# A state-space mixer on one core: the product for dt and the next chunk's front work placed sooner in the order of half steps

## The chip, the cores and the metric

One core of a Trainium2 chip runs the whole kernel. The metric is the device time of one execution in microseconds. PE is the matrix engine (PEld its weight loads), DVE the vector engine, ACT the engine of activation functions, POOL the general engine, SP the engine that issues nearly all DMAs here. Each engine works through its own instructions in order and waits for the others by semaphores.

## The reference, cut to what matters

The input is 8 sequences of 512 tokens with 512 features, all float32. One decoder layer is computed: a state-space mixer, attention to a second input, and a mixture of 32 experts, with a layer norm after each. The change lies in the mixer:

```python
xz = xn @ in_proj_w;  x_main, z = split(xz)              # 1024 channels each
x_main = silu(causal_conv4(x_main))
dt, B_ssm, C_ssm = split(x_main @ x_proj_w)              # 32, 16, 16 columns
dt = softplus(dt @ dt_proj_w + dt_proj_b)                # 1024 channels
h = exp(A * dt) * h + dt * B_ssm * x_main                # step by step over the tokens, 16 states a channel
y = (sum over states of h * C_ssm + x_main * D) * silu(z)
out = y @ out_proj_w + residual
```

## The kernel before

**Chunks and half steps.** The mixer goes through 16 chunks: 8 sequences, each in two halves of 256 tokens (t=0 and t=1). In a chunk the 1024 channels are 8 tiles of 128, taken in four pairs q = 0 to 3; the 16 states are four groups g. So a chunk has 4 x 4 = 16 pair steps, each of two half steps; k = 0 to 31 counts the half steps, and pair q begins at k = 8q. A pair step multiplies dt*x by B (L453, DVE), scans (L460, DVE, one instruction over 128x2056), and in each of its half steps multiplies by C (L478, DVE) and adds up the states on PE into `py` (L482, "collect"). The decays exp(A*dt) (L436, ACT, eight a pair step) are made one pair step ahead. `h` has two buffers, so the multiplication of a pair step needs the collects of the one but last.

**What a pair needs first.** `prepare(q)` makes dt and dt*x for a pair: four matmul records for `ps_dt` (L390), softplus on ACT (L400 to L406), four DVE operations (L410 to L413), two ACT scalings of x by D (L416) and eight DMAs on SP that lay dt and dt*x out as `both` (L424). The first decays of a pair read `both` two half steps before the pair begins, the first L453 when it begins. Before the change `prepare` for the next pair stands at k = 8q + 2; at the last pair it is that of the next chunk's pair 0.

**What else runs in a chunk.** At k = 1 and 2 `back` multiplies the gated output of the chunk before by the out projection (L511), and its norm follows. At k = 3 to 6 `gate_x` projects z (L303), at k = 7 comes its silu. The next chunk's input is loaded at k = 5 and normed at k = 9; `flip_x` transposes it, `convolve` projects and convolves one channel pair (L303, ACT L323 and L329, DVE L337), silu follows, and `x_proj` makes dt, B and C (L360). Weights for `back`, `gate_x` and `convolve` come in pieces of 512 KB through two buffers `wm` (L263, SP): asking for one piece starts the load of the next. All their PSUM tiles share the two slots of tag `mm`.

**Side units.** Attention and the router of the sequence before (and keys and values of the next) are cut into small units with weights in PE microseconds. `work(k)` gives the mixer's own weight of a half step; at each half step units are taken from the list as long as their sum stays within the share of the whole. So a change of `work` also moves units. Among them: `keys` (DVE L696), `maximum` (PE L774, DVE L776), `weigh` and `gather`, `hidden`, and `pick` and `choose` for the router (L547; DVE L554 to L610 with one exponential on ACT, L557).

**Order.** A step's function issues its first engine's work and returns the rest, which is issued by the next `settle`, one step later; `dry` issues all that is left. A planner then fixes each engine's order when the program is built: it keeps to the program's order by and large, but lets work that it counts as ready pass work that it counts as waiting. `silu` is kept in the program's order, with the table loads around it.

```python
    def do(fn, *args, first=False):
        if first:
            dry()
        rest = fn(*args)
        settle()
        if rest:
            left.append(rest)
```

Of the kernel before, what the change touches and what calls it, by code (L numbers as in the profile page):

```python
# [81 lines left out]
def layers(ctx, tc, a, x1d, filld, based, xbuf):  # L82
# [111 lines left out]
    first = cp.tile([P, E], F32, name="l_first")  # L194
    nc.gpsimd.iota(first, pattern=[[CAP, E]], base=-SLOTS, channel_multiplier=0, allow_small_or_imprecise_dtypes=True)
    first = first.unsqueeze(1).to_broadcast([P, SC, E])
# [154 lines left out]
    def silu(*tiles):  # L351

        for v in tiles:
            tc.keep_in_program_order(nc.scalar.activation(v, v, AF.Silu))
        tc.keep_in_program_order(nc.scalar.preload_act_table_set(LN_EXP))
# [16 lines left out]
    def bcast(f, g):  # L372

        got = []
        for r0 in (g * NG, NST + g * NG):
            t = bcp.tile([P, NG // 2, T], F32, tag="bc", name="bc")
            for r in range(2):
                n0 = r0 + r * NG // 2
                nc.sync.dma_start(
                    t[r * HP : (r + 1) * HP], f["scr"][n0 : n0 + NG // 2, :].partition_broadcast(HP)  # L380
                )
            got.append(t.unsqueeze(1))
        return got
# [47 lines left out]
    def decays(q, g, dt, da):  # L431

        for i in range(2):
            for n in range(NG):
                j, m = n // 2, n % 2
                nc.scalar.activation(  # L436
                    da[:, i * NG + n, 1:], dt[:, i, j, :], AF.Exp, scale=aneg[:, 2 * q + i, j, g, m : m + 1]
                )

    def carry(t, q, g):  # L440

        h = p3.tile([P, 2 * NG, T + 1], F32, tag="h", name="h", bufs=2)
        nc.scalar.copy(h.rearrange("p (i n) t -> p i n t", i=2)[:, :, :, 0], last(q, g) if t else none)  # L443
        return h
# [4 lines left out]
    def scan(t, q, g, dtx, bc, da, h):  # L449

        steps = h.rearrange("p (j m) t -> p j m t", m=NG // 2)[:, :, :, 1:]
        both = [P, 4, NG // 2, T]
        nc.vector.tensor_tensor(  # L453
            steps,
            dtx.rearrange("p i j t -> p (i j) t").unsqueeze(2).to_broadcast(both),
            bc[0].to_broadcast(both),
            ALU.mult,
        )
        flat = h.rearrange("p n t -> p (n t)")
        nc.vector.tensor_tensor_scan(flat, da.rearrange("p n t -> p (n t)"), flat, 0.0, ALU.mult, ALU.add)  # L460
        if t < S // T - 1:
            nc.vector.tensor_copy(last(q, g), h.rearrange("p (i n) t -> p i n t", i=2)[:, :, :, T])  # L462
# [27 lines left out]
    def gated(q, f, py):  # L490

        f["xs"].pop(q)
        pair = f["zs"][:, 2 * q : 2 * q + 2, :]
        nc.vector.tensor_tensor(pair, pair, py, ALU.mult)
# [167 lines left out]
    def sources(b):  # L662

        st, todo = {}, []

        def begin():
            load("Wv")
            st["cT"] = cT = quad("s2", "cT")
            nc.sync.dma_start(cT, rows(a["ctx"][b]))
            st["mk"] = mk = p1.tile([P, S], U8, tag="mk", name="mk")  # L670
            nc.sync.dma_start(mk, a["mask"][b : b + 1, :].to_broadcast([P, S]))
            kept[b] = [dp.tile([S, D], F32, tag="vd", name="vd"), dp.tile([D, S], F32, tag="kd", name="kd")]

        def values(pc):
            if pc == 0:
                load("Wk")
            w, cT = loaded["Wv"], st["cT"]
            ps = dense(lambda dc: cT[:, dc, pc * P : (pc + 1) * P], lambda dc: w[:, dc, :])

            def put():  # L680
                v = p3.tile([P, D], F32, tag="row", name="v")
                nc.scalar.copy(v, ps)
                nc.sync.dma_start(kept[b][0][pc * P : (pc + 1) * P, :], v)

            return put

        def keys(oc):
            if oc == 0 and b:
                load("Wq")
            w, cT = loaded["Wk"], st["cT"]  # L690
            ps = dense(lambda dc: w[:, dc, oc * P : (oc + 1) * P], lambda dc: cT[:, dc, :])

            def put():

                k = p3.tile([P, D], F32, tag="row", name="k")
                nc.vector.scalar_tensor_tensor(k, ps, bk[:, oc : oc + 1], st["mk"], ALU.add, ALU.mult)  # L696
                nc.sync.dma_start(kept[b][1][oc * P : (oc + 1) * P, :], k)

            return put

        todo.append((0, begin, False))
        for j in range(SC):
            todo.append((3.4, lambda j=j: values(j), False))
        for j in range(DC):
            todo.append((3.4, lambda j=j: keys(j), False))
        return todo
# [284 lines left out]
    def settle():  # L991

        got = [part() for part in left]
        left[:] = [x for x in got if x]

    def dry():
        while left:
# [10 lines that stand above are left out]

    def work(k):

        front = 6.9 if k in (1, 2) else 3.4 if 3 <= k < 7 or k in (12, 15, 18, 21, 24) else 1.0 if k in (11, 26) else 0.0
        return 1.2 + front

    f = {}
# [16 lines left out]
    for i, (b, t) in enumerate(chunks):  # L1031
        nf = {}
        after = chunks[i + 1] if i + 1 < len(chunks) else None
        if t == 0:
            side, spent = units(b - 1) if b else sources(0), 0.0

            own = [work(k) for k in range(len(steps))] * 2
            whole = sum(own) + sum(x[0] for x in side)
        py = None
        for k, (q, g, ci) in enumerate(steps):  # L1040
            if ci == 0:
                if (q, g) != (CC // 2 - 1, NST // NG - 1):
                    bcn = bcast(f, (g + 1) % (NST // NG))
                else:
                    bcn = bcast(nf, 0) if after else None
            if ci == 0:
                h = carry(t, q, g)

                if k + 2 < len(steps) or after:
                    nq, ng, _ = steps[(k + 2) % len(steps)]  # L1050
                    decays(nq, ng, (f if k + 2 < len(steps) else nf)["ready", nq][0], das[(n + 1) % 2])
                scan(t, q, g, f["ready", q][1], bc, das[n % 2], h)
                n += 1
            if k % 8 == 0:
                if k:
                    gated(q - 1, f, py)
                elif old:
                    gated(CC // 2 - 1, old[2], old[3])
                py = psy.tile([P, 2, T], F32, tag="py", name="py")
            if k == 0 and old:  # L1060
                twice_x(*old[:3])
            if k in (1, 2) and old:
                do(back, k - 1, *old[:3], first=True)
            if 3 <= k < 7:
                do(gate_x, k - 3, f, first=(k == 3))
            if k == 7:
                dry()
                silu(f["zs"])
            if k % 8 == 2:
                if q + 1 < CC // 2:  # L1070
                    do(prepare, q + 1, f)
                elif after:
                    do(prepare, 0, nf)
            if after:
                if k == 5:
                    load_x(*after, nf)
                if k == 9:
                    norm_x(nf)
                if k == 11:
                    for j in range(DC // 2):  # L1080
                        do(flip_x, j, nf)
                if k in (12, 15, 18, 21):
                    do(convolve, after[1], (k - 12) // 3, nf, first=(k == 12))
                if k == 23:
                    dry()
                    silu(*nf["xs"].values())
                if k == 24:
                    do(x_proj, nf)
            if side and (k >= 3 or t and k == 0):
                at = t * len(steps) + k + 1  # L1090
                while side and spent + sum(own[:at]) <= whole * at / len(own):
                    w, fn, alone = side.pop(0)
                    spent += w
                    do(fn, first=alone)
            settle()
            collect(2 * q + ci, g, h, bc, py, f)
            if ci == 1:
                bc = bcn
            if i < 2 and k % 2:
                clear(i * E // 2 + k // 2)  # L1100
        while t and side:
            _, fn, alone = side.pop(0)
            do(fn, first=alone)
        old = (b, t, f, py)
        f = nf
# [322 lines left out]
```

## Time and profile before

| | us |
|---|---|
| median of three runs | 5627.29 (5623.35 to 5629.95) |
| profiled execution | 5630.07 |
| its span, first to last instruction | 5628.4 |
| first scan of the mixer, last scan | 83.7, 3732.1 |
| chunks with t=0, from the third sequence on (4, 6, ..., 14) | 228.7 to 236.4 each |
| chunks with t=1 (3, 5, ..., 13) | 238.5 to 243.4 each |
| one scan (L460), one multiplication by B (L453), by C (L478) | 4.44, 2.29, 1.22 |
| mean granted TensorE clock | 0.937 |

The span is that of one profiled execution; 1.7 us of that execution lie outside it. The mixer phase with attention and router beside it takes about two thirds of it, the experts the rest. Chunks are counted from 0 and begin where their first scan begins.

### The profile page before, as it was taken

The numbers are of one execution on the slowest core, as the hardware profiler recorded it, in microseconds if no ns is written. First come the engines' busy times: TensorE is split into PE (matmuls) and PEld (weight loads), VectorE is DVE, ScalarE is ACT, GpSimd is POOL, SyncE is SP. The second block draws the span as 40 slices with busy tenths as digits, with TensorE's granted clock in tenths as the row PEclk, the third lists the DMA queues.
The fourth block names the chain that finished last, engine by engine and source line by source line (L and its number), as shares of the span: only waits on it lengthen the run. The fifth ranks groups of instructions, "written<-read, shape, count | busy, mean of one in ns | idle before, by whom it ended". The sixth has DMA issues, their size and how long they took to land. (4 is left out here: it accounts for less than half of the span.)

```text
span 5628.4 us, 59369 instructions
## 1 busy us (share of the span) xinstructions
PE 4884.2 (87%) x19752; PEld 2733.3 (49%) x19752; DVE 4299.8 (76%) x5098; ACT 2494.3 (44%) x5186; POOL 546.4 (10%) x424
## 2 busy tenths in 40 slices
PE   5667889888888988888898898879899999999994
PEld 3334334434434433443443343333577777777773
DVE  5988888999889888988888988854456555555554
ACT  4454555555555555455554555523122222222223
POOL 0100002000200200200020020010111111111111
PEclk8888999999998999999999899989899999999997
DMA  6767345443634534544363454431344444444444
GB/s 203 215 209 214 96 127 180 126 119 111 207 94 120 183 110 124 161 146 112 108 215 85 130 180 117 116 115 47 135 124 125 123 119 125 125 124 125 117 119 138
DMA packets 560419, 769.78 MB, mean 137 GB/s; under 512 B 135754, under 2 KB 268394, under 8 KB 560112
## 3 DMA queue, kind: packets, MB, share of 16 engines
q1 hardware_dynamic: 522608, 680.70, 40.0%
q0 software_dynamic: 33280, 76.90, 7.0%
q10 hardware_dynamic: 4224, 8.39, 0.4%
q8 instruction: 157, 2.57, 0.2%
q14 instruction: 150, 1.23, 0.1%
HBM read 508.68 MB, written 165.05 MB: 120 GB/s over the span
## 5 line engine op out<-in xcount | busy, mean ns | idle before, releaser
L460 DVE TENSOR_TENSOR_SCAN h<-l_da,h 128x2056 f32<-128x2056 f32 x256 | 1135.8, 4437 | 14.3 <-ACT h L443 2.1
L436 ACT ACTIVATE l_da<-both,l_aneg 128x256 f32<-128x256 f32 x2048 | 867.4, 498 | 563.8 <-DVE h L460 517.2
L482 PE MATMUL py<-h,l_twice 128*64 128x256 f32 x4096 | 632.2, 413 | 132.0 <-DVE h L478 131.6
L453 DVE TENSOR_TENSOR h<-both,bc 128x2048 f32<-128x2048 f32 x256 | 584.3, 2287 | 140.0 <-PE py L482 75.9
L478 DVE TENSOR_TENSOR h<-h,bc 128x1024 f32<-128x1024 f32 x512 | 611.8, 1219 | 5.3 <-DVE l_state L462 0.6
L482 PEld LDWEIGHTS py<-h,l_twice 128*64 128x64 f32 x4096 | 305.3, 145 | 486.8 <-issue 213.2
L1208 PE MATMUL ps_h<-xT,w 128*128 128x320 f32 x1536 | 435.9, 433 | 0.0
L776 DVE TENSOR_REDUCE mx<-ps_s 128x2 f32<-128x1024 f32 x256 | 310.7, 1217 | 126.3 <-PE ps_s L774 123.8
L774 PE MATMUL ps_s<-l_ka,l_qa 64*128 64x512 f32 x1024 | 312.4, 686 | 79.1 <-DVE mx L776 67.1
L1288 POOL DMA_INDIRECT based<-y,xe x160 | 249.4, 1559 | 1317.1 <-ACT y L1311 577.6
L800 PE MATMUL ps_t<-l_qa,l_ka 64*128 64x512 f32 x1024 | 302.3, 664 | 70.2 <-ACT eT L804 35.9
L1208 PEld LDWEIGHTS ps_h<-xT,w 128*128 128x128 f32 x1536 | 292.6, 191 | 118.4 <-issue 0.8
L1229 DVE TENSOR_TENSOR hT<-ps_h,p 128x320 f32<-128x320 f32 x128 | 62.9, 491 | 374.4 <-PE ps_h L1208 374.3
L804 ACT ACTIVATE eT<-ps_t 128x1024 f32<-128x1024 f32 x256 | 259.3, 1013 | 152.9 <-PE ps_t L800 152.8
L816 PE MATMUL po<-eT,l_va 128*64 128x512 f32 x1024 | 294.1, 646 | 27.8 <-ACT eT L804 22.9
L303 PE MATMUL ps_z<-xnT,wm 128*128 128x256 f32 x1024 | 256.1, 407 | 37.8 <-DMA wm<-in_in_proj_w 36.2
L1208 PE MATMUL ps_h<-t,s 128*128 128x320 f32 x1024 | 286.1, 432 | 0.0
L511 PE MATMUL po<-wm,zs 128*128 128x512 f32 x512 | 244.5, 629 | 37.9 <-DMA wm<-in_out_proj_w 37.6
L649 POOL DMA_INDIRECT xbuf<-x2t,dest x128 | 209.7, 1638 | 672.4 <-DVE l_state L462 319.3
L711 PE MATMUL ps_p<-x2T,wa 128*128 128x512 f32 x512 | 251.8, 641 | 5.7 <-ACT x2T L878 5.4
L303 PE MATMUL ps_x<-xnT,wm 128*128 128x256 f32 x1024 | 245.4, 394 | 10.7 <-DVE xr L864 10.0
L303 PEld LDWEIGHTS ps_z<-xnT,wm 128*128 128x128 f32 x1024 | 203.1, 203 | 95.8 <-issue 53.6
(224 smaller groups left out, 7259.6 us busy)
## 6 DMA issues: line engine op xcount, KB each, us to landing
bc<-scr SPq DMA_DIRECT2D x1024, 128.0 KB
w<-in_w SPq DMA_DIRECT2D x96, 1024.0 KB
wm<-in_in_proj_w SPq DMA_DIRECT2D x128, 512.0 KB
xbuf<-zero SPq DMA_DIRECT2D x32, 1362.5 KB
xe<-xbuf SPq DMA_DIRECT2D x32, 1362.5 KB
both<-dt SPq DMA_DIRECT2D x256, 128.0 KB
both<-dtx SPq DMA_DIRECT2D x256, 128.0 KB
wm<-in_out_proj_w SPq DMA_DIRECT2D x64, 512.0 KB
```

Source lines behind the costliest of these rows:

```text
L303: nc.tensor.matmul(ps[:, i, :], w[:, dc, i * P : (i + 1) * P], f["xnT"][:, dc, :], start=(dc == 0), stop=(dc == DC - 1),)
L436: nc.scalar.activation(da[:, i * NG + n, 1:], dt[:, i, j, :], AF.Exp, scale=aneg[:, 2 * q + i, j, g, m : m + 1])
L453: nc.vector.tensor_tensor(steps, dtx.rearrange("p i j t -> p (i j) t").unsqueeze(2).to_broadcast(both), bc[0].to_broadcast(both), ALU.mult,)
L460: nc.vector.tensor_tensor_scan(flat, da.rearrange("p n t -> p (n t)"), flat, 0.0, ALU.mult, ALU.add)
L478: nc.vector.tensor_tensor(steps, steps, bc[1].to_broadcast([P, 2, NG // 2, T]), ALU.mult)
L482: nc.tensor.matmul(py[j * HP : (j + 1) * HP, c % 2, :], twice, h[:, j * 2 + m, 1:], start=False, stop=(s == (NST // NG - 1, NG // 2 - 1, 1)),)
L774: nc.tensor.matmul(ps[:, j, :], qa[r, lt * P : (lt + 1) * P], ka[r, :], start=True, stop=True)
L776: return lambda: nc.vector.tensor_reduce(mx[:, lt, :].unsqueeze(2), ps, AX.X, ALU.max) and None
L800: nc.tensor.matmul(ps[:, j, :], ka[r, kc * P : (kc + 1) * P], qa[r, :], start=True, stop=True)
L804: nc.scalar.activation(eT, ps, AF.Exp)
L816: nc.tensor.matmul(po[j * 2 * HD : (j + 1) * 2 * HD, :], va[:, kc, i, j * HD : (j + 2) * HD], eT[:, j, :], start=(kc == 0), stop=(kc == SC ...
L1208: nc.tensor.matmul(ps, w[:, n, r * P : (r + 1) * P], x[:, n, :], start=not more and n == 0, stop=n == 1, skip_group_check=more,)
```

## The change

`prepare` goes from k = 8q + 2 to k = 8q, ahead of `back` in the first pair. For the next chunk the flips go from k = 11 to 10, the four convolutions from 12, 15, 18, 21 to 11, 13, 15, 18, the silu from 23 to 20 and `x_proj` from 24 to 21; with `prepare` at k = 24 the next chunk's first dt product follows three half steps behind it instead of two. `work` is written anew to match: 1.0 for each `prepare`, which counted only at k = 26 before.

```diff
     def work(k):
 
-        front = 6.9 if k in (1, 2) else 3.4 if 3 <= k < 7 or k in (12, 15, 18, 21, 24) else 1.0 if k in (11, 26) else 0.0
+        front = 6.9 if k in (1, 2) else 3.4 if 3 <= k < 7 or k in (11, 13, 15, 18, 21) else 1.0 if k == 10 or k % 8 == 0 else 0.0
         return 1.2 + front
...
-            if k % 8 == 2:
+            if k % 8 == 0:
                 if q + 1 < CC // 2:
                     do(prepare, q + 1, f)
                 elif after:
...
-                if k == 11:
+                if k == 10:
                     for j in range(DC // 2):
                         do(flip_x, j, nf)
-                if k in (12, 15, 18, 21):
-                    do(convolve, after[1], (k - 12) // 3, nf, first=(k == 12))
-                if k == 23:
+                if k in (11, 13, 15, 18):
+                    do(convolve, after[1], (11, 13, 15, 18).index(k), nf, first=(k == 11))
+                if k == 20:
                     dry()
                     silu(*nf["xs"].values())
-                if k == 24:
+                if k == 21:
                     do(x_proj, nf)
```

## The prediction

> **What bounds the kernel now.** I began with the busy line of the page, then cut the span at the first scan of each chunk and read the windows.
>
> ```profile
> PE 4884.2 (87%) x19752; PEld 2733.3 (49%) x19752; DVE 4299.8 (76%) x5098; ACT 2494.3 (44%) x5186; POOL 546.4 (10%) x424
> ```
>
> ```profile
> 1631.50:1874.90 243.40, 212.10 (x855) 101.77 (x854) 214.25 (x232) 133.50 (x271) 2.71 (x8) 0.91 0.40 116
> 1874.90:2105.50 230.60, 202.74 (x832) 96.10 (x830) 205.03 (x189) 121.06 (x256) 36.51 (x21) 0.97 0.52 159
> ...
> sum 2834.30, PE 2473.83 PEld 1182.49 DVE 2515.44 ACT 1527.13 POOL 222.59; mean PE 206.15 PEld 98.54 DVE 209.62 ACT 127.26 POOL 18.55
> ```
>
> The columns are window, length, busy PE, PEld, DVE, ACT, POOL, then the clock and DMA. The rows are a t=1 and a t=0 chunk; the sum is over the twelve chunks 3 to 14. In them DVE works 2515.4 of 2834.3 us and PE 2473.8. So the mixer phase is DVE work with 319 us of idle DVE, 26.6 us a chunk, and PE nearly as full. The change does not alter DVE's work; it can win or lose only idle DVE time. The expert phase after 3741 us is not touched. Next, DVE's waits between 688 and 3741 us (total, times, longest):
>
> ```profile
> DVE h L453 <- PE py L482: 68.1, 58, 2.7
> DVE mx L776 <- PE ps_s L774: 50.1, 32, 3.9
> DVE h L453 <- DMA both<-dtx: 48.2, 8, 7.8
> DVE xs L337 <- ACT xs L329: 41.8, 24, 3.0
> DVE g_m L558 <- ACT g_sc L557: 36.2, 6, 9.9
> ...
> DVE dtx L410 <- ACT dtx L406: 12.6, 8, 2.0
> ```
>
> The third row is the largest single stall that hangs on `prepare`. Six of its eight are about 7 us long and sit at one place, the change from channel pair 0 to pair 1 in the t=0 chunks 4 to 14; one of 4.7 us is in the last chunk. The timelines of DVE, SP and PE around one of them:
>
> ```profile
> 1919.05 0.68 DVE L413 TENSOR_TENSOR dtx<-dt,xs 128x512 f32<-128x512 f32 x1
> 1926.91 4.50 DVE L453 TENSOR_TENSOR h<-both,bc 128x2048 f32<-128x2048 f32 x2 [7.18 <-DMA both<-dtx]
> ```
>
> ```profile
> 1917.88 1.98 SPq L424 DMA_DIRECT2D both<-dt  x3
> 1920.71 0.37 SPq L523 DMA_DIRECT2D x1d<-o  x1
> 1921.12 0.60 SPq L424 DMA_DIRECT2D both<-dt  x1
> 1921.82 2.63 SPq L424 DMA_DIRECT2D both<-dtx  x4
> 1924.55 0.55 SPq L263 DMA_DIRECT2D wm<-in_in_proj_w  x1
> ```
>
> ```profile
> 1898.59 7.13 PE L511 MATMUL po<-wm,zs 128*128 128x512 f32 x16 [1.51 <-DMA wm<-in_out_proj_w]
> 1905.65 1.12 PE L390 MATMUL ps_dt<-xd,l_w_dt 32*128 32x256 f32 x4
> ...
> 1928.43 5.38 PE L303 MATMUL ps_z<-xnT,wm 128*128 128x256 f32 x16 [3.13 <-DMA wm<-in_in_proj_w]
> ```
>
> The dt product is queued on PE behind both halves of `back` (1905.65), so dtx is ready only at 1919.7. Its eight copies leave SP until 1924.45 and land by 1926.9. DVE has nothing else. The same eight issues hold up the weight piece for the last z projection, and PE starves for 3.13 us.
>
> **The change, part by part** (gains against the profiled execution, 5630.1 us). What is moved per `prepare`: four PE matmul records (1.12 us), seven ACT operations, four DVE operations of 0.69, 0.68, 0.68, 0.68 = 2.7 us, two ACT scalings and eight SP issues of 0.61 us = 4.9 us.
>
> (a) *dt product two half steps sooner at pair 1.* It passes `back` (2 x 7.13 us of PE), so its copies can be issued at least 14 us earlier and the 48.2 us go. What is late next: in chunk 8 the collects of pair step 2 end on PE at 1918.8, when DVE arrives at 1919.7, so there is just room. Further on DVE waits at `keys` (L696 on ps_p, 1.9 to 3.1 us). DVE gets there 7.2 us earlier; PE recovers its 3.13 us gap and 1.66 us of slow matmuls behind it (5.38 against 3.72 us for the same 16 records at 1918.83), 4.8 us. So 2.4 us come back in six chunks: 48 - 14 = **34 us gained**, bounds 0 and 48.
>
> The row first: after a 3.13 us gap those 16 matmuls took 5.38 us. [...]
>
> (b) *L410 on ACT*, 12.6 us: eight short stalls behind the exponentials of pair 1. At half step 0 DVE has other work, but the ACT chain is as long. **8 us**, bounds -10 (as long again as now) and 12.6.
>
> (c) *silu and the gate's exponential.* In the t=1 chunks the silu of the next chunk's xs (k=23) meets the gate's exp (issued at k=22). ACT then changes tables back and forth while DVE waits:
>
> ```profile
> 2301.19 1.28 ACT L354 ACT_TABLE_LOAD   x1
> 2302.49 0.63 ACT L354 ACTIVATE xs<-xs 128x512 f32<-128x512 f32 x1
> 2303.14 1.28 ACT L557 ACT_TABLE_LOAD   x1
> 2304.43 0.31 ACT L557 ACTIVATE g_sc<-g_sc 128x128 f32<-128x128 f32 x1
> 2304.76 1.28 ACT L354 ACT_TABLE_LOAD   x1
> ```
>
> With the silu at k=20, and the gate's product moved by the new weights from k=22 to k=23, they lie apart. Of six waits (36.2 us, most of them 5.3) I leave 2.5 us each for the exp and its hand-over: **21 us**, bounds 0 and 31. The row: each load took 1.28 us and the next operation followed 0.02 us later. [...]
>
> (d) *Start of t=1 chunks.* DVE waits there 2.3 to 3.9 us for ps_s (seven times, 23.9 us). The four DVE operations of `prepare` (2.7 us) now fall into that hole, but its matmuls put ps_s off by 1.1 us: 1.6 x 7 = 11, of which I take **8**, bounds 0 and 19.
>
> (e) *What it costs.* The eight copies now stand on SP in front of or among the out-projection weights of `back`; SP is in order, and what waits behind them is those pieces, then bc. PE already waits for these pieces 28.3 us in 12 times, 2.4 us each. A delay of 4.9 us, passed on in full in all 15 chunks with a `back`, is 74 us; none is 0. Between them I take the row's 2.4 us: **-36**. The PSUM slot costs nothing: ps_dt holds one of two `mm` slots that `back` needs, but ACT reads it in 1.4 us while PE runs the first half of the piece (1.8 us).
>
> (f) *Flips at k=10, convolutions at 11, 13, 15, 18, product at 21, the other prepares.* Counts stay; distances between neighbours shrink from three half steps to two or three, over 14 us of DVE, longer than a convolution's chain (3.7 us PE, 0.57 and 1.1 us ACT, 2.9 us DVE). The flips now have one half step instead of two behind the norm; PE may wait there for ACT, which t=1 chunks cover (PE has waits on DVE there) and which costs up to 2 us each otherwise. Their L337 stalls (41.8 us) change places; **0**, bounds -20 and +20. The weights add 3.0 to each chunk's own sum (360.4 to 366.4 a batch), which moves side units by one half step at most places: inside these bounds.
>
> Sum: 34 + 8 + 21 + 8 - 36 = 35 us. 5630.1 - 35 = 5595; the median of the runs lies 2.8 us below the profiled execution: **5592 us**.
>
> **Rivals.** *Slower: SP blocks the weights.* If SP has the eight copies ahead of a weight piece, it first waits for DVE's dt (L424 on L412: 91.9 us in 34 times, 2.7 each), then issues for 4.9 us: PE gets 7.6 us late, 15 times, 114 us. Against 71 us of gains that is +43: 5670 us. It decides from 71 / 15 = 4.7 us a chunk. For it: just this happened to the z piece at 1924.55. Against it: two of the four pieces are asked for early, and the order on SP is planned by readiness.
>
> *No change: the stall only moves.* PE is busy 206 of 236 us, and the collects have 0.9 us of room at the stall shown. If PE hands back all of (a) as waits at L453 and L696, the other 37 us of gains face 36 of (e): about 5626 us. For it: 68 us of waits on py, the largest row. Against: PE has two starved stretches here that go.
>
> **How the numbers follow.** Forecast 0.60, slower rival 0.25, no change 0.15. A difference under 0.2% (11 us) cannot be told from none. The low end takes (e) at half and (b) to (d) at their bounds: 5549; the range reaches up past no change into the better part of the slower rival, 5645. Faster 0.60 (the forecast), within 0.2% 0.13 and slower 0.27 (the slower rival, and 0.02 of the third case).
>
> **What would show it.** Right: the 7 us waits on both<-dtx gone; L558's wait under 3 us; L410's and the ps_s wait at t=1 starts smaller; PE's wait for wm ahead of L511 grown to about 5 us. Wrong: that wait above 7 us with DVE waiting on py behind it, or L696 and py rows grown by as much as both<-dtx lost.

## The result, and the profile after

The changed kernel is slower: a median of 5800.75 us over four executions (5790.71 to 5805.19) against 5625.32 us over four of the kernel before, a ratio of 1.0309 (95% interval 1.0291 to 1.0327). The profiled execution took 5805.2 us with a span of 5803.5. The forecast was 5592, the range ended at 5645; even the slower rival (5670) fell 130 us short.

The busy line of the page after, in the same columns as before:

```profile
PE 4914.3 (85%) x19752; PEld 2736.4 (47%) x19752; DVE 4290.3 (74%) x5098; ACT 2527.8 (44%) x5204; POOL 638.3 (11%) x424
```

DVE has the same 5098 instructions and as much work (4290.3 against 4299.8 us); PE has 30 us more for the same instructions (the 512 of the out projection, L511, alone 257.5 against 244.5). ACT has 18 instructions more, all table loads. So the 175 us are waiting time of DVE. The windows cut at the first scan of each chunk show where: two single chunks (t=1, t=0), and the sum over the same twelve chunks as before.

```profile
1694.90:1945.10 250.20, 201.39 (x842) 98.02 (x841) 210.85 (x226) 135.13 (x272) 13.89 (x8) 0.91 0.40 111
1945.10:2195.20 250.10, 214.80 (x845) 99.56 (x843) 207.17 (x195) 124.97 (x258) 37.93 (x21) 0.93 0.49 148
...
sum 2983.60, PE 2496.32 PEld 1184.95 DVE 2507.31 ACT 1559.37 POOL 308.45; mean PE 312.04 PEld 148.12 DVE 313.41 ACT 194.92 POOL 38.56
```

The twelve chunks grew from 2834.3 to 2983.6 us, 149 us; DVE's idle time in them grew from 318.9 to 476.3. Of the rest, 13.7 us lie in the chunks ahead of these twelve (chunk 3 begins at 701.8 instead of 688.1) and 12 in the last chunk and what follows it. DVE's waits in the mixer phase after (total, times, longest):

```profile
DVE h L453 <- PE py L482: 186.2, 50, 12.6
DVE g_m L554 <- PE ps_l L547: 62.0, 7, 10.8
...
DVE hT L891 <- PE ps_p L711: 50.2, 21, 2.7
DVE total L847 <- ACT r L846: 26.9, 7, 5.3
...
DVE dtx L410 <- ACT dtx L406: 4.8, 6, 0.9
...
DVE g_m L558 <- ACT g_sc L557: 2.6, 7, 0.4
```

What the change aimed at is gone: no wait on both<-dtx (48.2 before), L558 down from 36.2 to 2.6, L410 from 12.6 to 4.8. In its place stand py (68.1 before), the router's logits ps_l (2.0 before) and hT (L891), the hidden values of the expert that all tokens use, which are worked out beside the router. The ps_l row has six waits of about 10 us, one in each t=1 chunk. This is DVE's timeline ahead of one of them:

```profile
2388.77 0.16 DVE L54 TENSOR_SCALAR v<-mv 128x4 f32<-128x4 f32 x1
2388.84 2.28 DVE L453 TENSOR_TENSOR h<-both,bc 128x2048 f32<-128x2048 f32 x1
...
2391.12 2.28 DVE L453 TENSOR_TENSOR h<-both,bc 128x2048 f32<-128x2048 f32 x1
...
2393.39 4.43 DVE L460 TENSOR_TENSOR_SCAN h<-l_da,h 128x2056 f32<-128x2056 f32 x1
...
2397.79 4.43 DVE L460 TENSOR_TENSOR_SCAN h<-l_da,h 128x2056 f32<-128x2056 f32 x1
...
2402.20 1.21 DVE L478 TENSOR_TENSOR h<-h,bc 128x1024 f32<-128x1024 f32 x1
2403.33 0.15 DVE L77 SCALAR_TENSOR_TENSOR less<-mv,o 128x4 f32<-128x4 f32 x1
2403.41 3.48 DVE L478 TENSOR_TENSOR h<-h,bc 128x1024 f32<-128x1024 f32 x3
2417.65 0.29 DVE L554 TENSOR_REDUCE g_m<-ps_l 128x4 f32<-128x128 f32 x1 [10.76 <-PE ps_l L547]
```

L54 to L77 are the last steps of the layer norm ahead of the router: tiny operations on 128x4 values (0.15 us each). Here they take 14.6 us from the start of the first to the start of the last and begin at pair step 13: two multiplications, two scans and a C multiplication stand between them on DVE. In the kernel before they take 1.8 to 2.5 us in the t=1 chunks 3 to 13, at pair step 11, with the long operations behind them:

```profile
2275.92 0.17 DVE L54 TENSOR_SCALAR v<-mv 128x4 f32<-128x4 f32 x1
2277.60 0.16 DVE L59 TENSOR_TENSOR m<-v,r 128x4 f32<-128x4 f32 x1 [1.51 <-ACT r L57]
...
2278.40 0.16 DVE L77 SCALAR_TENSOR_TENSOR less<-mv,o 128x4 f32<-128x4 f32 x1
2278.58 4.50 DVE L453 TENSOR_TENSOR h<-both,bc 128x2048 f32<-128x2048 f32 x2
```

Everything of the router hangs on L77, and ACT and PE of the changed kernel show it in the same places of their timelines:

```profile
2403.52 2.93 ACT L79 ACTIVATE x2t<-x2t,less,o 128x512 f32<-128x512 f32 x4 [12.45 <-DVE less L77]
```

```profile
2403.47 1.11 PE L482 MATMUL py<-h,l_twice 128*64 128x256 f32 x2 [12.64 <-DVE h L478]
```

PE, which has the collects, the flips of x2t and the logits still to do, stands idle for 12.64 us, until DVE's first C multiplication behind the two scans; then it has more work than DVE, and DVE waits 10.76 us for it at L554 and 1.5 to 2.7 us at each L891 behind. The two engines work one after the other at the end of every sequence. This was not among my cases.

To read the experiments by place, here is DVE's idle time per pair step in us, the mean of six t=0 chunks (4 to 14) and of six t=1 chunks (3 to 13), worked out from the traces; the sum is over all 16 pair steps. Pair steps are counted from 0 and run from one scan to the next. Only idle stretches of more than 50 ns count, so the sums lie a little under the 318.9 and 476.3 us above.

| kernel | t=0: steps 2, 3, 4 | t=0: 9, 12, 14 | t=0 sum | t=1: step 3 | t=1: 13, 14, 15 | t=1 sum |
|---|---|---|---|---|---|---|
| before | 1.3, 7.2, 0.0 | 2.4, 1.5, 0.8 | 26.3 | 0.2 | 6.0, 0.1, 0.0 | 24.0 |
| after | 1.8, 9.9, 1.5 | 6.3, 4.3, 4.5 | 38.7 | 8.2 | 0.0, 0.0, 18.5 | 38.0 |
| p1_after_pinned | 0.1, 0.1, 10.6 | 6.0, 4.2, 4.2 | 32.3 | 8.5 | 0.1, 0.0, 0.7 | 24.7 |
| v3_pinned_sent_late | 4.9, 3.5, 2.0 | 6.5, 4.2, 4.3 | 32.4 | 1.1 | 0.5, 0.0, 0.6 | 20.8 |
| e5_prepare_1 | 4.2, 0.0, 10.5 | 2.4, 1.5, 0.8 | 28.6 | 8.7 | 5.9, 0.1, 0.0 | 27.7 |
| v1_prepare1_sent_late | 6.7, 0.2, 3.6 | 2.5, 1.5, 0.8 | 24.3 | 0.2 | 5.7, 0.1, 0.0 | 23.1 |
| e3_weights_only | 3.3, 4.5, 3.2 | 5.4, 3.8, 2.9 | 32.7 | 0.1 | 6.6, 0.1, 0.5 | 23.3 |

### The profile page after: what moved, and what is told of

Its sections match the earlier page's. It is cut to its first block, busy times and chain, and to the rows that moved or that the text cites. A ratio compares the mean times of both kernels' runs of the same rounds, so it can differ in the third digit from the quotient of the medians.

```text
span 5803.5 us, 59380 instructions
## 1 busy us (share of the span) xinstructions
PE 4914.3 (85%) x19752; PEld 2736.4 (47%) x19752; DVE 4290.3 (74%) x5098; ACT 2527.8 (44%) x5204; POOL 638.3 (11%) x424
## 5 line engine op out<-in xcount | busy, mean ns | idle before, releaser
L482 PE MATMUL py<-h,l_twice 128*64 128x256 f32 x4096 | 644.5, 424 | 307.6 <-DVE h L478 307.1
L649 POOL DMA_INDIRECT xbuf<-x2t,dest x128 | 219.5, 1715 | 973.8 <-DVE z L905 597.8
L511 PE MATMUL po<-wm,zs 128*128 128x512 f32 x512 | 257.5, 657 | 60.9 <-DMA wm<-in_out_proj_w 38.3
L303 PE MATMUL ps_z<-xnT,wm 128*128 128x256 f32 x1024 | 241.5, 391 | 36.7 <-DMA wm<-in_in_proj_w 27.1
L1208 PEld LDWEIGHTS ps_h<-t,s 128*128 128x128 f32 x1024 | 195.0, 190 | 80.6
```

What stands on the lines that cost most here:

```text
L303: nc.tensor.matmul(ps[:, i, :], w[:, dc, i * P : (i + 1) * P], f["xnT"][:, dc, :], start=(dc == 0), stop=(dc == DC - 1),)
L482: nc.tensor.matmul(py[j * HP : (j + 1) * HP, c % 2, :], twice, h[:, j * 2 + m, 1:], start=False, stop=(s == (NST // NG - 1, NG // 2 - 1, 1)),)
L1208: nc.tensor.matmul(ps, w[:, n, r * P : (r + 1) * P], x[:, n, :], start=not more and n == 0, stop=n == 1, skip_group_check=more,)
```

## The experiments

The ratios are each kernel's time over that of the kernel before, with 95% intervals.

**The parts one by one.** First pair 1's product alone, at k = 0 instead of 2:

```diff
-            if k % 8 == 2:
+            if k == 0 or k % 8 == 2 and k > 2:
```

> Before with prepare of pair 1 alone moved, from k=2 to k=0. Weights theory (the eight copies of dt and dt*x stand on SP ahead of the out-projection weights, PE starves in back, DVE waits at pair step 3): the extra idle time of DVE after the change at pair steps 1 and 3 comes back, 3.2 + 2.7 us in a t=0 chunk and 8 us in a t=1 chunk, 14 us a sequence, about 100 us in all: 5725 us. Norm theory (the planner splits the chain of the norm ahead of the router, ln3, by 14.7 us of other DVE work and sets the router's choose at pair step 15 instead of 13, so DVE is idle at the end of each sequence): the built order of this kernel has the chain whole and choose at step 13, as before, so none of that loss; the 48 us of waits on both<-dtx go: 5580 to 5625 us.

Measured 5660.74 us, 1.0076 (1.0052 to 1.0099), between the two expectations. The stall is gone, another has its place, which the kernel before does not have. DVE's waits, and SP's timeline at the same place of a t=0 chunk:

```profile
DVE st L73 <- DMA xt<-in_x: 57.0, 6, 11.0
```

```profile
1904.21 0.39 SPq L263 DMA_DIRECT2D wm<-in_out_proj_w  x1
1908.74 3.02 SPq L424 DMA_DIRECT2D both<-dt  x4
1911.86 3.38 SPq L424 DMA_DIRECT2D both<-dtx  x4
1915.35 1.00 SPq L263 DMA_DIRECT2D wm<-in_out_proj_w  x1
```

L73 is the norm of the next chunk's input, six times about 10 us at pair step 4 of the t=0 chunks. That input has the SBUF place of `back`'s output, so it is loaded only when `back` is through. And `back` is late: its last weight piece could be asked for when PE has used the second one, at 1907.6, but it stands on SP behind the eight copies, which first wait for DVE's dt until 1908.7, and leaves at 1915.35. In the t=1 chunks the same order shows as 8.7 us of idle time at pair step 3, 7.2 of them waits on py.

The other three moves of `prepare` alone (pairs 1 to 3 at k = 8q, the next chunk's pair 0 left at k = 26):

```diff
-            if k % 8 == 2:
+            if k % 8 == 0 and q + 1 < CC // 2 or k == 26:
```

> Before with the products of pairs 1, 2 and 3 moved from 8q+2 to 8q, the next chunk's pair 0 left at k=26. Weights theory: as with pair 1 alone, about 5725 us, no more. Norm theory: in the built order the ln3 chain is split by 14.7 us at pair step 12 and choose stands at step 14, half way to the changed kernel's 15: some 6 to 14 us a sequence, seven sequences, above the kernel with pair 1 alone by 40 to 100 us.

Measured 5824.06 us, 1.0361 (1.0334 to 1.0387): more than the whole change, and more than either theory said. The wait for the input is there (58.3 us), and the router's norm takes 14.7 to 15.8 us, with 87.7 us of waits of g_m on ps_l.

The front alone (flips, convolutions, silu and product as in the change, `prepare` and weights as before):

> Before with only the next chunk's front work sooner (flips 10, convolutions 11, 13, 15, 18, silu 20, x_proj 21); every prepare and the weights as before. Weights theory: no loss, 5600 to 5630 us (the gate's exponential gains up to 21 us). Norm theory: the ln3 chain is split by 14.7 us at step 11, but choose stays at step 13: between 0 and 90 us slower. Front theory (closer convolutions bunch PE work and DVE waits for it): most of the 175 us, over 5720 us.

Measured 5688.58 us, 1.0120 (1.0097 to 1.0143). The router's norm takes 16.6 to 18.3 us, and g_m on ps_l has 90.5 us. Here the chain begins at pair step 11 and the router's choice (L554) stands at 13, both as in the kernel before; with the chain split, pair step 13 of the t=1 chunks has 16.3 us idle instead of 6.0.

The change with the old weights of `work`:

> The changed kernel with the old work(k), so that the side units keep their old places by the balance. If the new weights, which put the side units of the t=1 chunks half a step to a step later, make the loss: near before, under 5660 us. If the moved steps themselves make it: 5750 to 5800 us. The built order has the ln3 chain split by 14.7 us at step 12 and choose at step 14, so by the norm theory about half of the loss at the sequence's end goes, some 60 us: 5740 us.

Measured 5881.49 us, 1.0463 (1.0439 to 1.0487), above every expectation. The norm chain takes 15.0 to 15.6 us. The new weights, which I put at nothing, are worth 1.54% (some 85 us) on top of the moves. And the new weights alone, on the kernel before:

> The kernel before with the new weights of work alone: no product, flip or convolution is moved. In the order that is built the router's norm chain of the t=1 chunks then has 6.6 us of other DVE work inside it (none before, 14.7 in the whole change), and the router's choice stays at pair step 13. Theory A, the split chain is what costs: half the split and no later choice cost 10 to 50 us, 1.002 to 1.009, shown as waits of x2t (L79) on less (L77) or of g_m on ps_l. Theory B, the split costs only where the choice is pushed to pair step 15: no difference, 0.998 to 1.002. Theory C, the weights by themselves are worth the 80 us that they were worth on top of the other moves: 0.985 to 0.995.

Measured 5662.88 us, 1.0061 (1.0044 to 1.0077). Inside A's band, but not by A's mechanism: the norm chain takes 6.4 us, yet the t=1 chunks lose nothing (23.3 against 24.0 us idle). The loss is in the t=0 chunks, 6.4 us each, where DVE now waits 5.4 us for py at pair step 9. So a chain split by 6.4 us cost the t=1 chunks nothing here.

**The router's norm kept in one piece.** From half step 24 of a t=1 chunk on, scans and C multiplications are issued on DVE behind the norm's last operation. Nothing else is touched.

```diff
+    behind = lambda k: tc.issue_after(pin["less"]) if "less" in pin and k >= 24 else nullcontext()
...
-                scan(t, q, g, f["ready", q][1], bc, das[n % 2], h)
+                with behind(k): scan(t, q, g, f["ready", q][1], bc, das[n % 2], h)
...
-            collect(2 * q + ci, g, h, bc, py, f)
+            with behind(k): collect(2 * q + ci, g, h, bc, py, f)
```

> The changed kernel with the scans and C multiplications from k=24 of the t=1 chunks behind the ln3 chain on DVE; in the built order the chain is whole at step 11 and choose at step 13, as before the change. Norm theory: the 18.5 us of idle DVE at step 15 of each t=1 chunk fall to 3 to 6, six or seven times 13 us or more: 5680 to 5720 us. What is left over before (60 to 100 us) is then the loss at steps 1 to 4 and in the t=0 chunks. If the norm is only a sign: over 5770 us.

Measured 5680.19 us, 1.0126 (1.0108 to 1.0143). The chain takes 1.5 us, at pair step 11 again, and two rows of DVE's waits read

```profile
DVE h L453 <- PE py L482: 105.2, 29, 6.8
...
DVE g_m L554 <- PE ps_l L547: 1.1, 1, 1.1
```

1.0309 - 1.0126 = 1.83% is 103 us of the 175. The t=1 chunks are back at 24.7 us of idle DVE (38.0 in the change). The pin does two things at once: it keeps the chain whole, and it sets it back from pair steps 13 to 15 to its old place at 11. The front alone, above, shows that the split costs without a later start; how much of the 103 us is the later start isn't told apart. The same on the front alone (pinned from k = 22):

> The front work alone moved (5689 us, +69), with the scans and C multiplications from k=22 of the t=1 chunks issued on DVE behind the last operation of the ln3 chain; nothing else differs. The built order then has the chain whole at step 10 and choose at step 12. Norm theory: the 69 us go, 5610 to 5640 us, and the waits of choose on ps_l (87 us in 6) and of the collects on DVE (up to 17.8 us) with them. If the split chain is only a sign of a PE that is late for other reasons, DVE now waits ahead of the chain instead and the time stays over 5670 us.

Measured 5649.82 us, 1.0072 (1.0054 to 1.0091): 0.48% of 1.20% came back, less than the norm theory said; the wait of g_m is gone (5.7 us left), but the moved front then makes DVE wait 8.5 us at pair step 10 of the t=1 chunks, most of it for ACT.

**Is the wait for the input one of order on DVE?** The norm of the input one half step later in the program (q1), or behind the scan of half step 10 (q4), in e5_prepare_1:

> Pair 1's product alone at k=0 (5661 us, +41), with the norm of the next chunk's input at k=10 instead of 9. In that kernel DVE no longer waits for both<-dtx but, in the same t=0 chunks, for the next input (st on xt<-in_x, 57 us in 6, up to 11.0). If this wait is just the next late thing: DVE does the work of step 4 first, 40 to 57 us go, 5605 to 5625 us. If PE is what is late there, the wait turns up at py or zs: 5645 us or more.

Measured 1.0079 (1.0057 to 1.0100), the row of L73 unchanged at 57.0 us: the planner put it back where it was.

```diff
-                if k == 9:
-                    norm_x(nf)
+                if k == 10:
+                    with tc.issue_after(one["scan"]): norm_x(nf)
```

> Pair 1's dt product at half step 0 alone, and the statistics of the next chunk's input (L73 and what follows) issued on DVE behind the scan of half step 10, one pair step later than the planner puts them. Theory A, the planner puts L73 on DVE before the input has landed, and the wait is one of order alone: the 57 us of L73 on xt go, nothing else grows by as much, and the 1.0076 falls to 0.998 to 1.002. Theory B, PE and the transfers behind it are late there and DVE must wait for them somewhere: the wait moves to py at L453 or to the first taps of the next convolutions (L337), and the ratio stays at 1.005 to 1.010.

Measured 5673.16 us, 1.0089 (1.0073 to 1.0106). L73 waits no more, and DVE's waits have a new row at pair step 4 of the t=0 chunks:

```profile
DVE zs L494 <- ACT v L682: 76.0, 6, 13.9
```

That is the gated product of pair 0, waiting for gates that PE came to late (the row names the last of several awaited; in chunk 8 PE itself waits 3.79 us there for a weight piece of the z projection). So it is not order on DVE: PE is late there, and DVE must wait for it somewhere. The same pin in the whole change, together with p1's:

> The whole change with both orders set by hand: the router's norm in one piece (as p1) and the next input's statistics behind the scan of half step 10 (as the run q4_prepare1_norm_pinned). Theory A, order on DVE is the whole of the loss but for SP's part at pair step 3 of the t=1 chunks (8 us, six times): from p1's 1.0126 to about 1.003. Theory B, the input's wait only moves: 1.010 to 1.014, with py at L453 grown from 105 us by as much as L73 loses.

Measured 5752.48 us, 1.0223 (1.0208 to 1.0239), worse than either expectation. It can't be used for or against them: in the change the flips stand at half step 10, so the later norm holds them up (PE ps_t L287 waits 82.3 us for ACT's normed input).

**Is it SP?** The eight copies on another queue. On ACT's:

> Pair 1's product alone at k=0 (5661 us, +41), with its eight copies issued from ACT instead of SP. Weights theory: the out-projection weights are no longer held up on SP, the 8.7 us of DVE waiting for py at step 3 of the t=1 chunks go (about 50 us in all) and so do the waits on bc (22 us): 5590 to 5620 us, PE's wait for wm ahead of L511 under 1 us each. Rival: the wait comes from the planned order on PE (the last collect records behind z projections): 5650 us or more, whatever queue the copies use.

Measured 5678.42 us, 1.0121 (1.0104 to 1.0138). Pair step 3 of the t=1 chunks has no idle time left and L73 waits 8.7 us instead of 57.0, which speaks for SP; but ACT now stands waiting with the copies, and the carries into `h` (L443) behind them cost DVE 60.3 us. On POOL's, and the weights there instead:

> The same, with pair 1's eight copies asked for on POOL's queue instead of the weights; on ACT's queue they took the 8.7 us of pair step 3 away, but ACT waited with them and 1.0121 came out. POOL has almost nothing else to do. Theory A: 0.994 to 1.001, pair step 3 of the t=1 chunks below 3 us idle. Theory B: 1.005 to 1.010. A third, that POOL's issues are slower and the copies land late: waits of DVE on both<-dtx of 5 us and more, 1.003 to 1.015.

Measured 5698.21 us, 1.0145 (1.0129 to 1.0161); pair step 3 of the t=1 chunks has 0.6 us idle, L73 waits 11.8 us. But in the t=0 chunks POOL issues the copies behind the scatter to the experts (L649): in chunk 8 the scatter takes it from 1902.7 to 1934.3 us, and ACT waits for dt:

```profile
1940.52 3.30 ACT L436 ACTIVATE l_da<-both,l_aneg 128x256 f32<-128x256 f32 x8 [21.93 <-DMA both<-dt]
```

DVE waits for the norm that ACT does behind it (L59 on L57), and the t=0 chunks stand idle 15.8 us at pair step 2, 1.3 in the kernel before.

> Pair 1's dt product at half step 0 alone (1.0076), with all projection weights (wm) asked for on POOL's queue, so that no copy stands ahead of them. Theory A, SP's order delays the weights and with them PE, the output projection, the next input and the gates: DVE's idle time at pair step 3 of the t=1 chunks falls from 8.7 us to below 3, the 57 us of waits for the input to below 15, and the ratio lies at least 0.6% under that of the kernel before with the same queue's own effect taken off, or near 1.000 if that queue by itself costs nothing. Theory B, PE is late of itself, by the dt product and by what it does ahead of the output projection: the waits stay, 1.005 to 1.010.

> The kernel before with all projection weights asked for on POOL's queue: what that queue does by itself. If SP's order costs nothing in the kernel before, 0.998 to 1.002. If SP holds weights up there too (the 3.13 us gap at the z projection and the stall behind it), 0.988 to 0.997. If POOL's issues come late or its transfers are slower, over 1.002, with PE's waits for wm (28 us before) grown.

Measured 1.0234 (1.0220 to 1.0248) with pair 1's product moved, 1.0237 (1.0215 to 1.0259) without. The queue itself costs 2.4%: the weights stand on POOL behind the scatter to the experts, which waits up to 165.7 us for the router (L649 on L643), and PE waits up to 27.6 us for a piece. With SP out of it, though, the moved product costs nothing (0.03% less), and pair step 3 has 0.5 us idle against 8.7. That holds for the t=1 chunks; in the t=0 chunks, where L73 still waits 58.9 us in all, the new wait covers the place.

So the last runs stay on SP and change its order alone: the eight copies are issued behind the output projection's last piece.

```diff
+                one["last"], nxt = one.get("wm"), p2.tile(...)      # in pieces()
+                one["wm"] = nc.sync.dma_start(nxt, src).ins
...
+            if k == 2:                     # behind back(1); send() issues pair 1's eight copies
+                with tc.issue_after(one["last"]): one["send"]()
```

> Pair 1's dt product at half step 0 alone, all on SP's queue, but its eight copies are issued behind the output projection's last weight piece, which stood behind them in e5_prepare_1. Theory A, that order was the whole cost: DVE's idle time at pair step 3 of the t=1 chunks falls from 8.7 us to below 3, the waits for the next input (57 us) to below 20, and since the copies still leave earlier than in the kernel before, part of its 48 us on both<-dtx is won: 0.993 to 0.999. Theory B, PE is late by the product itself: 1.005 to 1.010, waits as in e5_prepare_1. If the weights come in time but the copies land as late as before, 0.998 to 1.003.

Measured 5618.32 us, 0.9995 (0.9982 to 1.0008), twelve executions; theory A's band ended at 0.999. SP's timeline at the same place, and two rows of DVE's waits:

```profile
1880.69 3.80 SPq L263 DMA_DIRECT2D wm<-in_out_proj_w  x2
1885.23 3.46 SPq L424 DMA_DIRECT2D both<-dt  x4
```

```profile
DVE h L453 <- DMA both<-dtx: 5.0, 3, 3.9
...
DVE st L73 <- DMA xt<-in_x: 0.8, 1, 0.8
```

Both weight pieces leave ahead of the copies; from the end of pair 1's dt product to the end of `back` PE takes 19.9 us (1875.3 to 1895.2) instead of 25.7 (1898.8 to 1924.5 in e5_prepare_1). The 8.7 us and the 57 us are gone. So the copies' place on SP was the whole of the 0.76%. But the 48 us are not won either: in the t=0 chunks DVE now stands idle 6.7 us at pair step 2, most of it for py, and 3.6 at pair step 4 for the gates' silu (21.1 us in all).

In the whole change, with the norm in one piece:

> The whole change, with the router's norm kept in one piece (p1_after_pinned, 1.0126) and the eight copies behind the last weight piece. Theory A, p1's rest was this order for 0.8%, and the new weights' for 0.4 to 0.6% (t=0 chunks): 1.003 to 1.008, pair step 3 of the t=1 chunks below 3 us (8.5 in p1). Theory B: 1.010 to 1.014.

Measured 5663.19 us, 1.0069 (1.0048 to 1.0090). Another way to take the same cost out, pair 1's product back at k = 2:

> The whole change with the router's norm kept in one piece (the pin of p1), but with pair 1's dt product back at half step 2. Theory A, two separate losses (the split norm chain, which the pin has already given back, and pair 1's early product, which alone cost 0.76%): p1's 1.0126 falls to about 1.005, DVE's idle time at pair step 3 of the t=1 chunks falls from 8.5 us to below 2, and its wait for the next chunk's input (L73 on xt) from 67 us to below 20; the wait on both<-dtx comes back with some 48 us and takes back part of it. Theory B, what remains in p1 comes from the front's moves and the new weights, of which the front alone still lost 0.72% when pinned: it stays at 1.010 to 1.013.

Measured 5664.65 us, 1.0065 (1.0048 to 1.0081): the same. Its wait on both<-dtx did not come back (0.2 us), but pair steps 2 to 4 of the t=0 chunks have 10.2 us idle, 8.5 in the kernel before.

Last, v1 with the silu of the next chunk's xs behind the gate's exponential on ACT:

```diff
+                    with tc.issue_after(pin["exp"]) if t and "exp" in pin else nullcontext(): silu(*nf["xs"].values())
```

> v1_prepare1_sent_late, and in the t=1 chunks the silu of the next chunk's xs is issued on ACT behind the gate's exponential, so that ACT changes tables for it no longer while DVE waits. The wait of g_m on g_sc (35 us in 6, mostly 5.3) should fall to 2.5 us each, 15 us in all; gain over v1 0.1 to 0.35% if DVE has nothing else late there, none if the next chunk's x product (half step 24) becomes late instead.

Measured 5646.01 us, 1.0048 (1.0034 to 1.0063). The wait of g_m on g_sc fell as expected, from 34.3 to 16.6 us, and the kernel became 0.5% slower than v1: idle DVE grew by 2.8 us in each t=0 chunk, at pair steps 2 to 4 (3.4 us), and by 1.4 in each t=1 chunk, most of it at pair step 15. Why is open. No version was faster than the kernel before; v1 equals it.

**The sum.** Of the 3.09%, 1.83 are the norm chain, split and set later (p1), 0.57 the copies ahead of the weights (v3 against p1; their intervals don't overlap), and 0.69 remain. What remains lies in the t=0 chunks: from chunk 4 to 14 they are 48 us longer together than before, 37 of them idle DVE (32.4 against 26.3 us a chunk), while the t=1 chunks are 17 us shorter. Its largest place, 6.5 us at pair step 9, most of it waits on py, is that of e3_weights_only (5.4), so I put it down to the units that the new weights moved. Another 27.1 us (2.6 before) are waits of total (L847) on ACT's r, most of them at pair step 14: the silu now meets the division of the attention, and L845 has six table loads that the kernel before has not. Neither was taken away by itself. Why the new weights gain some 85 us on top of the moves and lose 35 alone stays open.

## Why the prediction was wrong

- **What bounds the kernel** was right: the work of DVE stayed the same and only its idle time moved.
- **(f) the moves of the front and the weights, 0 within 20 us.** This step failed most: 103 us for the norm chain, and a part, not measured by itself, of the 39 that remain. I counted operations and the distances between neighbouring steps, and checked whether each moved chain still fits. I did not ask what the planner makes of the new order. It let scans pass a chain of 0.15 us operations that nothing of the change touches. No single edit is to blame: `prepare`'s moves alone (e1) and the front's alone (e2) each split the chain, and the new weights alone (e3), which I counted inside the 20 us, cost 0.61% (34 us) at another place. Why the planner lets the scans pass is not shown.
- **(a) pair 1's product, 34 us gained.** The stall went as said. The working of what is late next stopped one step short: it followed DVE to L696, and the copies' own path on SP stood under (e) as a price, not as a delay of `back`, of the next input behind it and of the gates. With that order mended (v1) the time is that of before: PE's collects and ACT's gates were as late as the copies (10.4 us idle at pair steps 2 to 4 of a t=0 chunk, 8.5 before). That was the "no change" rival, true for this term.
- **(e) SP's copies, 36 us lost.** The cause was right, and so was the size: 45 us in the single edit (e5 against v1, 0.81%), 32 in the whole change (v3 against p1). That the size fits is partly luck: its 2.4 us a chunk were waits of PE that the kernel before has too, and these hardly grew (30.2 to 30.6 us); in e5_prepare_1 collects run between the pieces. The cost shows as py and as the next input instead. The slower rival had this mechanism at 114 us, three times its size; that it would be slower was right, the place of the loss was not.
- **(b) L410, 8 us gained:** the row fell by 7.8; what that was worth in time no run shows.
- **(c) silu and the gate's exponential, 21 us gained:** the row fell by 33.6, but the silu now meets L845 instead (total on r: 26.9 us), and v4 shows that 18 us less at this row need not shorten anything. Taking a row's total as time was the error.
- **(d) start of the t=1 chunks, 8 us gained:** nothing; pair step 0 has 3.9 us idle, 3.4 before.
- **The signs named:** of those for being wrong, the py row's growth came (118 us, against 48 lost at both<-dtx), but at other places than I meant; L696 left DVE's waits.
- **The table loads:** 1.28 us each in the prediction's rows; in the changed kernel too a load took 1.283 us by the profile's groups of instructions.

## What to carry to other kernels

Where an engine's order is planned over the whole program, a step moved earlier doesn't only carry its own work: the planner may order everything around it anew, and long operations can end up inside a short dependent chain elsewhere. After such a change, measure in the trace how long each serial chain takes from its first to its last operation (1.8 to 2.5 us against 14.6 here), and pin the chain before judging the move. For the moved step, list what each of its DMAs now stands ahead of on its queue, and follow that to the buffer it frees: here a weight piece, the output, and the next input that has the output's place.

## What the runs showed of the hardware

In the kernel before, the same sixteen matmuls took 7.13 us behind a gap of 2.18 us, and 8.83 us behind a shorter one of 2.07:

```profile
1662.04 8.83 PE L511 MATMUL po<-wm,zs 128*128 128x512 f32 x16 [2.07 <-DMA wm<-in_out_proj_w]
2136.33 7.13 PE L511 MATMUL po<-wm,zs 128*128 128x512 f32 x16 [2.18 <-DMA wm<-in_out_proj_w]
```

The granted clock in the trace tells these apart: its mean is 0.81 over the stretch of 8.83 us and 1.00 over that of 7.13. For the z projections in the prediction it is 0.68 over the 5.38 us behind the gap of 3.13, and 1.00 over the 3.72 us at 1918.83.

The clock records in the traces of before and after have the values 1.0 and 0.5 and no others. From 688 to 3700 us they have 64 and 76 stretches at 0.5. In each trace all of these begin on one grid of 3.413 us, within 0.01 us, and last whole slots of it, one to six. Counted over both traces, of 127 slots at full clock in which PE was busy for less than 44% of the time, 126 were followed by a slot at half clock; of 1364 in which it was busy for more than half, 4 were; in between, 10 of 29. What the clock goes by is not shown beyond these counts. The gap of 3.13 us in the prediction is among the 126: in the slot from 1926.27 to 1929.68 us PE was busy for 1.25 of 3.41 us, and the clock was 0.5 from 1929.68 us on, for 3.41 us.
